# Gate tiles by GpSimd's indirect gathers instead of SyncE's broadcast reads, in a convolution, attention and mixture-of-experts kernel

## The chip, the cores and the metric

The kernel runs on one core of a Trainium2 chip. A core has TensorE (PE; its weight loads are PEld), VectorE (DVE), ScalarE (ACT), GpSimd (POOL) and SyncE (SP), which only issues transfers, and 16 DMA engines that carry them. Every engine works through its own queue in order. The metric is the device time of one execution in microseconds. All times and durations below come from the profile of one execution, or from the list of measured times.

## The reference, cut to what matters

The input is 32 images of 128 channels with 56 x 56 points, in float32. Layer 0 is a convolution of signs with a residual; layer 1 turns each image into 3136 tokens of 128 channels, adds a linear attention, and then a mixture of 8 experts of which each token uses the best two. The last of these is the part that the change touches:

```python
def _L1_ffn_ref(x, router_w, router_b, expert_w, expert_b):
    router_probs = jax.nn.softmax(x @ router_w + router_b, axis=-1)
    top_p, top_i = jax.lax.top_k(router_probs, K)          # K = 2 of E = 8
    top_p = top_p / jnp.sum(top_p, axis=-1, keepdims=True)
    expert_out = jnp.einsum('bnd,edc->bnec', x, expert_w) + expert_b
    gathered = jnp.take_along_axis(expert_out, top_i[..., None], axis=2)
    return jnp.einsum('bnk,bnkc->bnc', top_p, gathered)
...
x = x + _L0_conv_ref(_gn(x), ...)                          # 3x3 convolution of signs
t = _to_tokens(x)                                          # 32 x 3136 x 128
t = t + _L1_attn_ref(_ln_t(t), ...)                        # q * sum(k * v)
t = t + _L1_ffn_ref(_ln_t(t), ...)
```

## The kernel before, in words

The kernel multiplies every token by all 8 experts, each time with the token first scaled by its gate for that expert, which is zero for six of the eight. PE then adds the eight products in PSUM, and no token has to be sorted to its expert.

The tokens of an image are cut into 25 chunks of up to 128, and these into 7 blocks: five of 512 tokens, one of 384 and one of 192. The experts are taken in 4 pairs. So an image has 28 steps of one block and one pair each. Per step:

- `spread` (L670 on) fetches a gate tile `bc`: the gates of the block for the two experts, one row of up to 1024 numbers, repeated in all 128 partitions (the channels). For the first pair of a block it also fetches `gt`, the same gates in bfloat16 parts, for the experts' biases (L676).
- `gated` (L689) multiplies the block's tokens `tt` by the gate tile on DVE.
- `experts` (L701, L707) multiplies the result by the two experts' weights on PE and accumulates in the PSUM tile `ff`.
- `finish` (L718, L721) adds `ff` to the tokens and stores the output.

The gates come from a chain earlier in the image. The statistics of the tokens go through a reciprocal root on POOL (L278, in `rstd_of`), DVE builds the logits (L562) and picks the two largest, PE transposes the gates (L621), ACT copies them (`gt_sb`), and SP writes them to a buffer `gp` in device memory (L628), where each block and expert has a row of 512 numbers. `gate_parts` writes the bfloat16 parts to `gb` with seven transfers (L643). The `bc` tiles are read back from `gp`, with a source that names the same bytes for every partition.

The order of the work comes from a list: each step is put at a time measured in images (`at(when, ...)`), with the stages of three to four images overlapped, and the steps are issued sorted by that time. A scheduler then settles the order of every engine's instructions and adds the waits. The times that matter here: an image's gates are written at s + 2.17 to s + 2.19; its 28 gate tiles are asked for from s + 2.235 on, each at the earliest when the multiply seven steps before it has been asked for, because `bc` has seven buffers; its multiplies start at s + 2.30 and take one image's time.

POOL has four jobs. For each image it takes two reciprocal roots (L278: one for the attention's normalisation, whose result ACT needs for `y`, one for the experts', whose result the logits need); it sets a column of ones in the seven tiles `y` (L386), each of which waits until PE has finished with an older one; and it adds the attention's bias to the tokens (`bias`, L464 and L469: seven and one instructions) once DVE has computed it (`kv_4`, `bq_kv`, L434). DVE's additions of the projected queries (`tok`, L518) need those sums. POOL issues no transfers.

Of the kernel before, what the change touches and what calls it, by code (L numbers as in the profile page):

```python
# [41 lines left out]
C = 128  # L42
# [3 lines left out]
N_EXP = 8  # L46
# [10 lines left out]
def conv_attn_moe_kernel(  # L57
# [19 lines left out]
    nc = tc.nc  # L77
# [9 lines left out]
    while c0 < n_ck:  # L87
        left = n_ck - c0
        n = PER if left > PER + 1 else (left + 1) // 2 if left > 3 else left
        blocks.append(list(range(c0, c0 + n)))  # L90
        c0 += n
    n_blk = len(blocks)
# [6 lines left out]
    def cols_of(b):  # L99
        return blocks[b][0] * C, min(n_tok, (blocks[b][-1] + 1) * C)  # L100

    const = ctx.enter_context(tc.tile_pool(name="const", bufs=1))
# [56 lines left out]
    def by_slot(name, *shape):  # L159
        both = [const.tile([C, *shape], F32, name=f"{name}{j}") for j in range(2)]  # L160
        for t in both:
            nc.gpsimd.memset(t, 0.0)
        return both
# [3 lines left out]
    lgp_all = by_slot("lgp", n_slot, N_EXP)  # L167
    n_half = 2
    gate_all = by_slot("gate", 2, n_half * C // (N_EXP * PER), N_EXP, PER)
    move_all = [const.tile([C, N_Q], F32, name=f"move{j}") for j in range(2)]  # L170

    def load_x(i: int):
# [107 lines left out]
    def plan_image(i: int):  # L280
        s = float(i)
        d = {}
# [93 lines left out]
        for g in range(n_blk):  # L376
            b = min(n_conv - 1, (cols_of(g)[1] - 1) // (ROWS * width))
# [292 lines left out]
        def spread(b, k):  # L670
            n = cols_of(b)[1] - cols_of(b)[0]
            if k == 0:
                gt = bpool.tile([n_g, WIDE], BF16, tag="gt", name=f"gt_{i}_{b}")
                rows = d["gb"][b, :, :, :n].rearrange("j e t -> (j e) t")
                for r in range(0, n_g, n_g // 3):
                    nc.sync.dma_start(gt[r : r + n_g // 3, :n], rows)  # L676
                d["gt", b] = gt
            bc = bpool.tile([C, 2, WIDE], F32, tag="bc", bufs=7, name=f"bc_{i}_{b}_{k}")
            nc.sync.dma_start(
                bc[:, :, :n],  # L680
                d["gp"][b, 2 * k : 2 * k + 2, :n].unsqueeze(0).to_broadcast([C, 2, n]),
            )
            d["bc", b, k] = bc

# [45 lines left out]
        for b in range(n_blk):  # L730
            for k in range(pairs):
                n = b * pairs + k
                at(max(s + 2.235 + 0.001 * n, begin + (n - 7 + 0.1) * unit), spread, b, k)
                at(begin + n * unit, gated, b, k)
                at(begin + (n + 1.3) * unit, experts, b, k)
            at(begin + ((b + 1) * pairs + 1.0) * unit, finish, b)
# [54 lines left out]
```

## Time and profile before

| what | value |
|---|---|
| time of the kernel before, median of 2 runs | 2791.74 us (2788.21 to 2795.28) |
| the profiled execution: its own time | 2786.31 us |
| the profiled execution: its span | 2784.5 us |
| mean granted clock of TensorE | 0.975 |
| bytes moved | 544.86 MB in 251246 packets |
| share of the 16 DMA engines, queue of SP | 55.9% (538.07 MB) |
| L679, issue of `bc` on SP | 896 times, median 349 ns |
| L689, multiply by the gate tile on DVE | 896 times, mean 1149 ns |
| L707, expert matmuls on PE | 3584 times, mean 551 ns |
| L278, reciprocal root on POOL | 64 times, mean 5326 ns |
| L464, bias add on POOL | 224 times, mean 1885 ns |

The span is the time from the first to the last instruction. "Busy" is the time in which an engine has an instruction running; a busy PE need not be at its peak. A line that ends in "<- engine, tile, line" names what an idle engine was waiting for, as the profile infers it from the semaphores. Issuing a transfer isn't counted as busy time.

### The profile page before, as it was taken

How to read it: one execution, taken by the hardware profiler on the slowest of the kernel's cores; microseconds unless marked ns; L12 is line 12 of the kernel's file. 1: busy time of each engine (PE TensorE's matmuls, PEld its weight loads, DVE VectorE, ACT ScalarE, POOL GpSimd, SP SyncE). 2: the span in 40 equal slices, each digit the busy share in tenths (PEclk: the TensorE clock that was granted, in tenths of full speed). 3: DMA queues.
4: the chain of work that ended last, by engine and by line, in shares of the span. 5: the costliest groups of instructions: out<-in, count | busy, mean ns of one | idle time of the engine just before them, and what ended most of it. 6: DMA issues, size and time to landing. Idle time of an engine off the chain costs nothing. (4 is left out here: it accounts for less than half of the span.)

```text
span 2784.5 us, 35742 instructions
## 1 busy us (share of the span) xinstructions
PE 2539.2 (91%) x11149; PEld 1537.5 (55%) x11149; DVE 2164.8 (78%) x5049; ACT 938.9 (34%) x2473; POOL 807.4 (29%) x568
## 2 busy tenths in 40 slices
PE   4799999999999999999999999999999999999887
PEld 2655555555555555555555555555555555555553
DVE  3578877788877788777879777888777888777875
ACT  3532333433333333333333333323334323333210
POOL 1322232232332232331332331332331332331320
PEclk9899999999999999999999999999999999999999
DMA  3166555466555466554566654575554575654566
GB/s 134 35 223 232 205 200 181 169 226 228 209 197 186 162 231 220 211 186 170 192 234 210 216 185 160 200 242 200 209 188 163 210 242 201 209 185 139 190 219 227
DMA packets 251246, 544.86 MB, mean 196 GB/s; under 512 B 54377, under 2 KB 147889, under 8 KB 251057
## 3 DMA queue, kind: packets, MB, share of 16 engines
q1 hardware_dynamic: 247424, 538.07, 55.9%
q10 hardware_dynamic: 3632, 4.51, 0.5%
q8 instruction: 90, 1.47, 0.2%
q14 instruction: 100, 0.81, 0.1%
HBM read 481.38 MB, written 61.08 MB: 195 GB/s over the span
## 5 line engine op out<-in xcount | busy, mean ns | idle before, releaser
L707 PE MATMUL ff<-gated,ew_sb 128*128 128x512 f32 (+2 forms) x3584 | 1513.9, 551 | 65.9 <-DVE gated L689 65.6
L689 DVE TENSOR_TENSOR gated<-tt,bc 128x1024 f32<-128x1024 f32 (+2 forms) x896 | 1025.3, 1149 | 33.5 <-PE ff L707 17.6
L707 PEld LDWEIGHTS ff<-gated,ew_sb 128*128 128x128 f32 x3584 | 644.1, 193 | 516.1 <-issue 339.0
L278 POOL TENSOR_TENSOR r<-var,m_half 128x28 f32<-128x28 f32 x64 | 340.0, 5326 | 1085.8 <-DVE var L277 1021.5
L464 POOL TENSOR_TENSOR tok<-tok,bq_kv 128x512 f32<-128x512 f32 (+2 forms) x224 | 415.1, 1885 | 206.3 <-DVE bq_kv L434 206.3
L328 PE MATMUL cv<-xb,w_bin 128*128 128x448 bf16 x2016 | 450.2, 358 | 1.4 <-DVE lgp L519 1.1
L498 ACT ACTIVATE qs<-q,r 128x136 f32<-128x136 f32 (+1 forms) x800 | 241.9, 370 | 463.4 <-issue 280.3
L389 ACT ACTIVATE y<-tok,r 128x128 f32<-128x128 f32 (+1 forms) x800 | 255.3, 394 | 226.6 <-POOL r L278 216.1
L400 PE MATMUL gram<-y 128*128 128x129 f32 (+1 forms) x1600 | 254.0, 297 | 77.1 <-ACT y L389 76.8
L489 PEld LDWEIGHTS q<-move,x 128*128 128x128 f32 (+1 forms) x1600 | 228.9, 191 | 123.9 <-issue 78.2
L328 PEld LDWEIGHTS <-w_bin 128*128 128x128 bf16 x2016 | 197.9, 98 | 166.4 <-issue 22.7
L400 PEld LDWEIGHTS gram<-y 128*128 128x128 f32 (+1 forms) x1600 | 228.9, 203 | 105.8 <-ACT y L389 90.1
L489 PE MATMUL q<-move,x 128*128 128x144 f32 (+1 forms) x1600 | 249.9, 291 | 3.8 <-DVE lgp L519 2.5
L562 DVE TENSOR_TENSOR logit<-logit,r 128x224 f32<-128x224 f32 x32 | 12.6, 393 | 296.9 <-POOL y L386 255.0
L367 DVE BATCH_NORM_STATS2 st<-tok 128x6 f32<-128x128 f32 (+1 forms) x800 | 182.4, 280 | 25.9 <-ACT tok L358 25.6
L339 DVE SCALAR_TENSOR_TENSOR x<-cv,alpha_col,x 128x448 f32<-128x448 f32 x224 | 151.5, 676 | 65.1 <-PE cv L328 61.2
L386 POOL MEMSET y<- 128x4 f32 x224 | 23.1, 104 | 608.4 <-PE gram L400 450.4
L718 DVE TENSOR_TENSOR tt<-tt,ff 128x512 f32<-128x512 f32 (+2 forms) x224 | 137.3, 613 | 68.9 <-PE ff L707 66.7
L518 DVE TENSOR_TENSOR tok<-tok,qs 128x384 f32<-128x384 f32 (+1 forms) x320 | 159.5, 499 | 37.6 <-ACT qs L498 31.4
L527 DVE BATCH_NORM_STATS2 st<-tok 128x6 f32<-128x128 f32 (+1 forms) x800 | 183.1, 282 | 0.0
L358 ACT COPY tok<-xt 128x512 f32<-128x512 f32 (+2 forms) x224 | 117.9, 527 | 180.2 <-PE xt L354 180.0
L665 PEld LDWEIGHTS l<-ident,tok 128*128 128x128 f32 (+1 forms) x800 | 106.8, 149 | 100.9 <-issue 78.2
(115 smaller groups left out, 1636.1 us busy)
## 6 DMA issues: line engine op xcount, KB each, us to landing
bc<-gp SPq DMA_DIRECT2D x640, 512.0 KB
x<-in_x_dram SPq DMA_DIRECT2D x64, 784.0 KB
bc<-gp SPq DMA_DIRECT2D x128, 384.0 KB
out_dram<-tt SPq DMA_DIRECT2D x64, 512.0 KB
bc<-gp SPq DMA_DIRECT2D x128, 192.0 KB
out_dram<-tt SPq DMA_DIRECT2D x32, 448.0 KB
gt<-gb SPq DMA_DIRECT2D x480, 24.0 KB
gb<-gt_parts SPq DMA_DIRECT2D x224, 24.0 KB
```

The costliest lines, as they stand in the source:

```text
L278: nc.gpsimd.tensor_tensor(dst, var, m_half.to_broadcast([C, n_slot]), ALU.pow)
L328: nc.tensor.matmul(cv, lhsT=w_bin[:, t, :], rhs=xs[:, b * ROWS + dy : b * ROWS + dy + ROWS, dx : dx + width], start=(t == 0), stop=(t == T ...
L367: nc.vector.bn_stats(st[:n, slot[c], :], d["tok"][:n, c, :])
L389: nc.scalar.mul(y[:n, j, :C], d["tok"][:n, c, :], d["r1"][:n, slot[c] : slot[c] + 1])
L400: nc.tensor.matmul(d["gram"], lhsT=y[:n, j, :C], rhs=y[:n, j, :], start=(c == 0), stop=(c == n_ck - 1),)
L464: nc.gpsimd.tensor_tensor(t, t, over, ALU.add)
L489: nc.tensor.matmul(p[:n, k, :], lhsT=d["x"][:, c * C : c * C + n], rhs=move, start=True, stop=True,)
L498: nc.scalar.mul(qs[:n, k, :], p[:n, k, : C + N_EXP], d["r1"][:n, slot[c] : slot[c] + 1])
L518: nc.vector.tensor_add(t, t, qs[:n, k:m, :C])
L527: nc.vector.bn_stats(st2[:n, slot[c], :], d["tok"][:n, c, :])
L689: nc.vector.tensor_tensor(g[:, :, :n], d["tt"][:, lo:hi].unsqueeze(1).to_broadcast([C, 2, n]), d.pop(("bc", b, k))[:, :, :n], ALU.mult,)
L707: nc.tensor.matmul(d["ff", b][:, :n], lhsT=ew_sb[:, e * C : (e + 1) * C], rhs=g[:, j, :n], start=False, stop=(e == N_EXP - 1),)
```

## The change

The gate tile of a step is no longer read by SP with a repeating source. GpSimd issues an indirect gather in its place: each of the 128 partitions names the row of `gp` that it wants, and gets that row. `gp` is looked at as rows of 1024 numbers, one for each block and pair, so all 128 partitions name the same row. The row numbers stand in a new constant tile `row_no`, a column for each of the 28 steps, which POOL fills at the start. A gather fetches the whole row of 1024 numbers, also for the two shorter blocks, whose tiles were read with 2 x 384 and 2 x 192 numbers before. The number of buffers and the times at which the tiles are asked for stay. From the first insertion on, lines of the changed kernel have numbers higher by 4, and after the second by 7 (`gated` is at L696, `experts` at L708 and L714).

```diff
     gate_all = by_slot("gate", 2, n_half * C // (N_EXP * PER), N_EXP, PER)
+
+    row_no = const.tile([C, n_blk * N_EXP // 2], mybir.dt.uint32, name="row_no")
+    for n in range(n_blk * N_EXP // 2):
+        nc.gpsimd.memset(row_no[:, n : n + 1], n)
     move_all = [const.tile([C, N_Q], F32, name=f"move{j}") for j in range(2)]
...
             bc = bpool.tile([C, 2, WIDE], F32, tag="bc", bufs=7, name=f"bc_{i}_{b}_{k}")
-            nc.sync.dma_start(
-                bc[:, :, :n],
-                d["gp"][b, 2 * k : 2 * k + 2, :n].unsqueeze(0).to_broadcast([C, 2, n]),
+            n_pair = b * (N_EXP // 2) + k
+            nc.gpsimd.indirect_dma_start(
+                out=bc.rearrange("p j t -> p (j t)"),
+                out_offset=None,
+                in_=d["gp"].rearrange("b (k j) t -> (b k) (j t)", j=2),
+                in_offset=bass.IndirectOffsetOnAxis(ap=row_no[:, n_pair : n_pair + 1], axis=0),
             )
             d["bc", b, k] = bc
```

## The prediction

> **What bounds the kernel now.** I read the page's busy times first, then the waits, and then one image in the middle of the run, engine by engine.
>
> ```profile
> PE 2539.2 (91%) x11149; PEld 1537.5 (55%) x11149; DVE 2164.8 (78%) x5049; ACT 938.9 (34%) x2473; POOL 807.4 (29%) x568
> ```
>
> PE comes first. The 32 images overlap; the pairs of reciprocal roots on POOL (L278) start at 1028.16, 1111.46 and 1195.99 us, so one image takes about 84 us. POOL works 25.5 us of each. The stretches inside one image (columns: length, then busy time of PE, PEld, DVE, ACT, POOL with counts, PE clock, DMA share, GB/s):
>
> ```profile
> 1136.00:1147.00 11.00, 11.00 (x73) 8.56 (x73) 6.11 (x20) 2.24 (x6) 0.42 (x4) 1.00 0.58 167
> 1142.00:1152.00 10.00, 10.00 (x47) 5.90 (x47) 7.90 (x18) 1.44 (x3) 2.35 (x4) 1.00 0.90 287
> 1150.00:1164.00 14.00, 12.98 (x44) 6.45 (x43) 13.85 (x18) 1.14 (x5) 14.00 (x8) 1.00 1.03 387
> 1164.00:1195.00 31.00, 31.00 (x129) 17.72 (x128) 29.68 (x82) 12.32 (x32) 0.02 (x1) 1.00 0.60 203
> ```
>
> See three things. DVE is as full as PE from 1150 to 1195 (43.5 of 45 us), so what holds DVE up there holds up the image. DVE has a hole from 1136 to 1147, where the new image's gate tiles are on their way. From 1150 to 1164 POOL and the DMA engines are full too. The timeline of POOL for that image, with the idle time before each group in brackets:
>
> ```profile
> 1111.46 10.67 POOL L278 TENSOR_TENSOR r<-var,m_half 128x28 f32<-128x28 f32 x2 [31.97 <-DVE var L277]
> ...
> 1139.18 0.10 POOL L386 MEMSET y<- 128x4 f32 x1 [2.61 <-PE gram L400]
> ...
> 1149.86 13.44 POOL L464 TENSOR_TENSOR tok<-tok,bq_kv 128x512 f32<-128x512 f32 x7 [6.24 <-DVE bq_kv L434]
> 1163.26 0.76 POOL L469 TENSOR_TENSOR tok<-tok,bq_kv 64x128 f32<-64x128 f32 x1
> 1195.99 5.92 POOL L278 TENSOR_TENSOR r<-var,m_half 128x28 f32<-128x28 f32 x1 [31.97 <-DVE var L276]
> ```
>
> POOL has two free stretches, 1122 to 1150 and 1164 to 1196, with 14.2 us of bias adds between them. Its results are waited for:
>
> ```profile
> DVE logit L562 <- POOL y L386: 255.0, 27, 9.4
> ...
> DVE gated L689 <- DMA bc<-gp: 15.0, 14, 8.7
> ```
>
> The first is the wait for the roots (named after the memset behind them), 9.4 us an image. The second is all that DVE now loses to gate tiles that come late, 8.7 of its 15.0 us in the last image. SP's timeline shows why:
>
> ```profile
> 1136.05 0.39 SPq L628 DMA_DIRECT2D gp<-gt_sb  x1
> 1137.41 3.77 SPq L643 DMA_DIRECT2D gb<-gt_parts  x7
> 1141.28 1.14 SPq L676 DMA_DIRECT2D gt<-gb  x3
> 1142.47 1.77 SPq L679 DMA_DIRECT2D bc<-gp  x4
> ```
>
> The first gate tile is issued 6.4 us after gp, behind ten other issues.
>
> **What the Trainium skill says.** *DMA: Bandwidth & Descriptors*, "Latency and other measured facts", gives a DMA from GpSimd about 1 us to its first byte, put down to the descriptors that its cores emit, against 0.6 us from SP; its section "Anatomy of one DMA — SWDGE (gpsimd) path" fits a GpSimd DMA as 2.0 us plus bytes over 436 GB/s. No DMA here is issued on POOL, so the trace can't confirm it; on SP one issue takes 0.35 us, and in the last image the first gate tile, issued at 2726.55, is used at 2730.71, 4.2 us later, with three more behind it. *GPSIMD Engine Reference*, "Performance pitfalls for Q7 kernels", prices small reads such as one per gather index at about 102 cycles each. *SBUF — State Buffer*, "Who interferes with whom", says a VectorE instruction with two SBUF inputs contends with a GpSimd instruction that reads SBUF. The trace agrees: the seven bias adds take 8.17 us in the first image (85.45 us), when no gate multiply runs, and 13.44 us beside them, and a multiply takes up to 1.90 instead of 1.21 us there.
>
> **The change part by part.**
>
> *Removed from SP:* 28 issues an image, 28 x 0.35 = 9.8 us of SP, and their waits for a free buffer. Nothing waits for SP alone, so 0. The output stores and gt loads are no longer queued behind those waits: 0 to a few us in all, taken as 0.
>
> *Row numbers:* 28 memsets of one column at the start. Eight like them (L244) take 0.33 us, so about 1.2 us near 9 us, where POOL then idles until 66: 0. Without that cover, 1.2 us once.
>
> *Bytes:* a gather always fetches 4 KB a partition, also for the blocks of 384 and 192 columns: 28 x 512 = 14336 KB against 20 x 512 + 4 x 384 + 4 x 192 = 12544 KB, 1.84 MB more an image, 59 MB in all. These are the last eight gathers; at 387 GB/s they are 4.7 us of DMA time in a stretch where the engines are 0.60 busy: 0.
>
> *Emission on POOL, the unknown.* Call it E for one gather of 128 rows. Low end: 0.35 us, SP's row. High end: 128 x 102 cycles at 1.2 GHz, an estimate from the GPSIMD page, 10.9 us, if the row numbers are read one by one. The DMA page's 1 us is for a plain DMA; this one must also read 128 row numbers, one in each partition, while VectorE uses two inputs. I take E = 1.5 us and keep 0.8 to 2.6 for the range. POOL's sum is 25.5 + 28 x 1.5 = 67.5 of 84 us: it fits on average, and is full at E = (84 - 25.5) / 28 = 2.1 us. What matters is the order on the queue.
>
> *POOL's new order in an image:* the two roots; the last gather of the image before; the memsets of y, the last of which ends at 1139.3; gathers 0 to 10; two bias adds; gather 11; the other bias adds; gathers 12 to 26 with two memsets between; the next two roots. Gather n waits until multiply n - 7 has freed its buffer. I replay this on the old times. gp, issued at 1136.05, has landed by 1139.3 (the same fit gives its 128 KB 2.3 us). Multiplies 0 to 3 end early enough that gathers 7 to 10 hardly wait, so gather 10 ends at 1139.3 + 11E. The bias inputs (L434, ready at 1149.8 now) come some 4 us later, since DVE's new order puts six gate multiplies ahead of kv (L431), still before 1155.8. Two adds, gather 11, the other adds and gather 12: 1139.3 + 13E + 14.2. With the page's 2.0 us and 524288 bytes at 436 GB/s (3.2 us), tile 12 is there at 1156.7 + 13E. Multiply 12 (block 3, first pair) starts at 1173.30 now. At E = 1.28 it is just in time; at 1.5 it lands at 1176.2, 2.9 us late. DVE has 1.3 us of idle time up to 1195; the other 1.6 us reach the roots, and through them y and PE. PE's own lead over this tile hides only its direct wait. Later gathers need one tile in about 2.9 us and catch up.
>
> *The roots wait behind gather 26*, which waits for multiply 19 (ends 1194.4, root input ready 1195.9): 1194.4 + 1.5 = 1195.9, so 0 now; each further us of E goes into the 9.4 us wait. DVE's logit, ACT's y and then PE's gram wait for that.
>
> *Contention:* a multiply beside POOL's reads grew by up to 0.69 us. If every gather did that, 28 x 0.69 = 19 us an image; if it reads only its numbers, 0. I take 1 us.
>
> *Early start:* gather 0 starts at 1139.3 instead of 1142.47. DVE's new order fills its hole with these multiplies, but PE is full there and the chain through kr (L444, L445) ends as late as before, so I count 0 in the middle. At the end nothing covers: 3 us are gained once.
>
> Sum: 1.6 + 1.0 = 2.6 us an image, over the 31 images with a successor 81 us, less 3: 2786.31 + 78 = 2864 us in terms of the profiled execution (span 2784.5 and 1.8 around it). The median of the runs shown is 5.4 above that one, so I forecast 2869.
>
> **The rivals.**
>
> *POOL becomes the bound.* From E = 2.1 on POOL has no free time, and the late tile shows sooner: at E = 2.6, tile 12 lands at 1190.5, 17 us late, and POOL's sum is 98.3 us an image: 14.3 to 17 us x 31, 3230 to 3310 us. At 2.1 it is 10.7 - 1.3 = 9.4 us an image, 3080. For: POOL issues in order, bias and roots are waited for. Against: 71% of POOL is idle.
>
> *Emission is short, and the early start pays.* One mechanism: tile 0 leaves SP's queue of ten issues behind it. It decides where E is at most 1.2, so that tile 12 is in time. Then up to 65.6 us of PE's waits for a gate multiply (46 times) and the 15.0 us of DVE can go; half of that, 40 us, gives 2752, the whole 2711. For: DVE's hole and the full DMA engines after it. Against: PE's work is 79 of 83.5 us already.
>
> *The transfer is hidden either way.* With E from 1.2 to 1.35 the lateness fits into DVE's idle 1.3 us and the numbers cancel: about 2790, within the 2% that a measurement of this kernel can tell from no change.
>
> *It isn't one descriptor a row:* if rows are cut into smaller pieces, emission is several times longer and the first rival holds with 4000 us and more.
>
> **How the numbers follow.** Forecast (E 1.35 to 1.9; 2815 to 3030): 0.42. POOL the bound: 0.24, with pieces 0.03. Hidden: 0.22. Early start: 0.09, of which 0.05 are faster by over 2%. Slower by over 2% gathers the forecast's upper 0.40 and 0.27: 0.67; within 2%: 0.28; faster: 0.05. The range leaves out about a tenth at each end: 2760 to 3240.
>
> **What would show it.** Gathers on POOL at about 1.5 us; a bias group that starts near 1156 and is split by one gather; idle time of DVE before multiply 12 for a DMA, some 2 to 3 us an image; DVE's wait for the roots no longer than 9.4 us; no SP issues of bc. I am wrong if E is under 1.2 or over 2, if the multiplies lengthen much beyond 1.21 us, or if gathers land slower than 3.2 us after emission.

## The result, and the profile after

The changed kernel takes 2978.85 us (median of 2 runs, 2978.28 to 2979.41) against 2791.74 us (2788.21 to 2795.28). The ratio is 1.067, with a 95% interval of 1.061 to 1.073: 187 us slower, 6 us an image. The forecast was 2869 us, 78 us slower: the sign and the range were right, the size was not. The profiled execution took 2978.28 us, with a span of 2976.5 us, 192 us longer than before. One execution of one experiment below (the product of `gt` last) ran in a slow state, 4195 us at a mean clock of 0.585, and is left out of that experiment's median.

The page of the changed kernel, its engines' busy times and the groups of the gathers and of the multiplies (busy us and mean ns, then the idle time before them):

```profile
PE 2583.9 (87%) x11149; PEld 1558.6 (52%) x11149; DVE 2245.8 (75%) x5049; ACT 940.3 (32%) x2473; POOL 1730.9 (58%) x1492
...
L684 POOL DMA_INDIRECT bc<-gp,row_no x896 | 1087.1, 1213 | 689.7 <-DVE gated L696 348.1
L696 DVE TENSOR_TENSOR gated<-tt,bc 128x1024 f32<-128x1024 f32 (+2 forms) x896 | 1145.9, 1283 | 223.3 <-DMA bc<-gp,row_no 114.2
```

PE executes the same 11149 instructions, but is busy 44.7 us longer; the mean granted clock fell from 0.975 to 0.962. The other 147 us of the longer span are idle time of PE. DVE executes the same 5049 instructions and is busy 81 us longer. One image in four stretches (length, busy time of PE, PEld, DVE, ACT, POOL, then PE clock, DMA share and GB/s):

```profile
1127.00:1142.00 15.00, 12.63 (x54) 7.42 (x53) 9.33 (x16) 0.85 (x2) 12.03 (x10) 1.00 0.91 293
1142.00:1155.00 13.00, 10.25 (x42) 5.35 (x41) 12.96 (x15) 1.72 (x6) 12.56 (x11) 1.00 0.53 190
1155.00:1189.00 34.00, 34.00 (x144) 19.34 (x143) 32.32 (x89) 12.34 (x32) 17.27 (x17) 1.00 0.79 259
1189.00:1200.00 11.00, 8.00 (x32) 5.62 (x30) 0.93 (x3) 5.76 (x14) 10.80 (x4) 0.84 0.41 167
```

The stretch that the forecast worried about, the long one from 1155 on, is the healthy one: PE is full there. PE has its holes in the first 28 us, while the gathers and then the bias adds run, and at the roots, where the clock falls too. POOL's timeline for this image, with the idle time before each instruction in brackets:

```profile
1127.00 0.94 POOL L684 DMA_INDIRECT bc<-gp,row_no  x1 [0.99 <-DMA gp<-gt_sb]
1128.24 0.94 POOL L684 DMA_INDIRECT bc<-gp,row_no  x1 [0.30 <-issue]
...
1143.53 2.50 POOL L468 TENSOR_TENSOR tok<-tok,bq_kv 128x512 f32<-128x512 f32 x2
1146.18 1.76 POOL L684 DMA_INDIRECT bc<-gp,row_no  x1 [0.16 <-issue]
1147.97 5.07 POOL L468 TENSOR_TENSOR tok<-tok,bq_kv 128x512 f32<-128x512 f32 x5
1153.00 1.42 POOL L473 TENSOR_TENSOR tok<-tok,bq_kv 64x128 f32<-64x128 f32 x1
1154.58 0.96 POOL L684 DMA_INDIRECT bc<-gp,row_no  x1 [0.16 <-issue]
...
1187.19 2.18 POOL L684 DMA_INDIRECT bc<-gp,row_no  x1 [0.30 <-DVE gated L696]
1189.39 4.82 POOL L282 TENSOR_TENSOR r<-var,m_half 128x28 f32<-128x28 f32 x1
```

A gather takes 0.94 us when nothing disturbs it, with 0.30 us to the next. The five bias adds after 1147.97 are of three sizes; those of 128x512 take 1.27 us each, where in the kernel before the median of this size was 2.24 us. DVE at the same time:

```profile
1147.95 6.16 DVE L696 TENSOR_TENSOR gated<-tt,bc 128x1024 f32<-128x1024 f32 x1
```

One multiply, which takes 1.21 us elsewhere, takes 6.16 us: it starts with the first of POOL's six adds and ends 1.1 us after the fifth. In the kernel before, the adds run one behind the other too (13.44 us for seven), but there is no such multiply; there adds and multiplies took turns. POOL's first two adds of that image ran from 1149.86 to 1152.04 and from 1152.00 to 1154.25, and each multiply below ends 1.1 us after one of them:

```profile
1151.22 1.90 DVE L689 TENSOR_TENSOR gated<-tt,bc 128x1024 f32<-128x1024 f32 x1
...
1153.44 1.90 DVE L689 TENSOR_TENSOR gated<-tt,bc 128x1024 f32<-128x1024 f32 x1
```

And what PE waits for in the changed kernel (total us, times, longest):

```profile
PE gram L404 <- ACT y L393: 112.1, 49, 4.7
PE l L669 <- ACT tt L672: 34.8, 27, 1.8
PE ff L708 <- DMA gt<-gb: 34.4, 16, 12.6
...
PE ff L708 <- issue: 19.0, 11, 4.3
```

The wait for `gt`, the experts' bias gates, was 6.9 us in all before. Here it is 34.4, and 19.0 more stand before the same matmul. The wait for `y`, which hangs on the roots, was 76.8 us.

### The profile page after: what moved, and what is told of

Same layout as the page of the kernel before. It is cut to its first block, busy times and chain, and to the rows that moved or that the text cites. A ratio compares the mean times of both kernels' runs of the same rounds, so it can differ in the third digit from the quotient of the medians.

```text
span 2976.5 us, 36136 instructions
## 1 busy us (share of the span) xinstructions
PE 2583.9 (87%) x11149; PEld 1558.6 (52%) x11149; DVE 2245.8 (75%) x5049; ACT 940.3 (32%) x2473; POOL 1730.9 (58%) x1492
## 3 DMA queue, kind: packets, MB, share of 16 engines
q0 software_dynamic: 129024, 469.82, 46.3%
## 4 chain that ended last, share of the span: by engine, by line
PE 44%; DVE 18%; ACT 12%; POOL 9%; issue 9%; DMA 8%; SPq 1%; another core or an unknown queue 0%; DVEq 0%; ACTq 0%; POOLq 0%
PE ff L714 23%; DVE gated L696 8%; PE cv L332 8%; POOL r L282 6%; PE q L493 5%; DMA bc<-gp,row_no 4%; ACT y L393 4%; PE gram L404 3%; POOL bc L684 3%; ACT xb L297 3%; ACT qs L502 2%; DMA gt<-gb 2%; DVE tok L522 2%; PE xt L358 2%; ACT xb L313 1%
## 5 line engine op out<-in xcount | busy, mean ns | idle before, releaser
L714 PE MATMUL ff<-gated,ew_sb 128*128 128x512 f32 (+2 forms) x3584 | 1541.9, 557 | 30.7 <-DVE gated L696 17.6
L684 POOL DMA_INDIRECT bc<-gp,row_no x896 | 1087.1, 1213 | 689.7 <-DVE gated L696 348.1
L696 DVE TENSOR_TENSOR gated<-tt,bc 128x1024 f32<-128x1024 f32 (+2 forms) x896 | 1145.9, 1283 | 223.3 <-DMA bc<-gp,row_no 114.2
L714 PEld LDWEIGHTS ff<-gated,ew_sb 128*128 128x128 f32 x3584 | 658.0, 197 | 483.8 <-issue 387.0
L332 PE MATMUL cv<-xb,w_bin 128*128 128x448 bf16 x2016 | 433.8, 356 | 1.0 <-DVE lgp L523 0.8
L404 PE MATMUL gram<-y 128*128 128x129 f32 (+1 forms) x1600 | 264.9, 301 | 112.3 <-ACT y L393 112.1
L282 POOL TENSOR_TENSOR r<-var,m_half 128x28 f32<-128x28 f32 x64 | 306.8, 4805 | 72.0 <-DVE var L281 71.4
L404 PEld LDWEIGHTS gram<-y 128*128 128x128 f32 (+1 forms) x1600 | 236.8, 208 | 149.0 <-ACT y L393 127.2
L468 POOL TENSOR_TENSOR tok<-tok,bq_kv 128x512 f32<-128x512 f32 (+2 forms) x224 | 261.5, 1198 | 44.9 <-DVE bq_kv L438 44.0
L669 PE MATMUL l<-ident,tok 128*128 128x128 f32 (+1 forms) x800 | 142.2, 297 | 35.1 <-ACT tt L672 34.8
```

Of the source, the lines that this page charges most:

```text
L282: nc.gpsimd.tensor_tensor(dst, var, m_half.to_broadcast([C, n_slot]), ALU.pow)
L332: nc.tensor.matmul(cv, lhsT=w_bin[:, t, :], rhs=xs[:, b * ROWS + dy : b * ROWS + dy + ROWS, dx : dx + width], start=(t == 0), stop=(t == T ...
L404: nc.tensor.matmul(d["gram"], lhsT=y[:n, j, :C], rhs=y[:n, j, :], start=(c == 0), stop=(c == n_ck - 1),)
L468: nc.gpsimd.tensor_tensor(t, t, over, ALU.add)
L684: nc.gpsimd.indirect_dma_start(out=bc.rearrange("p j t -> p (j t)"), out_offset=None, in_=d["gp"].rearrange("b (k j) t -> (b k) (j t)", j= ...
L696: nc.vector.tensor_tensor(g[:, :, :n], d["tt"][:, lo:hi].unsqueeze(1).to_broadcast([C, 2, n]), d.pop(("bc", b, k))[:, :, :n], ALU.mult,)
```

## The experiments

In each run the kernel before was timed beside the others; its medians were 2789.55 to 2792.35 us. Times below are medians, ratios are against it. "Held" is DVE's time above the usual duration (the median of the same instruction in the kernel before without the bias adds), summed over all of DVE's instructions that are over it by 0.2 us or more: 121 us before, 218 us after the change, 0 in both kernels without the adds.

### The bias adds: one at a time, and none

In the changed kernel, one gather's step between any two bias adds:

```diff
+        unit_b = 1.0 / (n_blk * N_EXP // 2)
-            at(s + 1.445 + 0.001 * g, bias, g)
+            at(s + 1.445 + unit_b * g, bias, g)
```

> The changed kernel, with the bias adds of an image set one unit apart, so that a gather stands between any two of them on POOL; nothing else is edited. Theory A (the group of five bias adds holds one gate multiply for about 5 us, in 31 images): the multiplies of 6.2 to 6.6 us go, none is over 3 us, and the time falls by 100 to 155 us, to 2825 to 2880. Theory B (DVE and PE wait at the start of an image for tiles that DVE's new order puts first): the long multiplies may go, but PE's work only moves up to the next wait, and the time stays within 25 us of 2979. Theory C (POOL's queue is too slow with 28 gathers, and roots and tiles come late): no change or slower, since each gather behind a bias add now starts later: 2970 to 3020.

Measured: 2908.96 us, ratio 1.043 (1.040 to 1.046), 70 us less than the change alone, which lies between the numbers of theories A and B: the adds are one cost of several. POOL now does what the edit says:

```profile
1108.05 1.27 POOL L468 TENSOR_TENSOR tok<-tok,bq_kv 128x512 f32<-128x512 f32 x1
1109.48 1.84 POOL L685 DMA_INDIRECT bc<-gp,row_no  x1 [0.16 <-issue]
1111.34 1.27 POOL L468 TENSOR_TENSOR tok<-tok,bq_kv 128x512 f32<-128x512 f32 x1
```

No multiply is longer than 3 us any more (33 were, 167 us above the usual in sum), and DVE is held for 167 us. So the run of adds costs about 70 us, a bit over a third of the change.

Then both kernels with the adds left out, so that the tokens are not given the attention's bias:

```diff
-            at(s + 1.445 + 0.001 * g, bias, g)
+            pass
```

> The changed kernel without the bias adds on POOL (they are left out; their vector is zero with these inputs). Theory A: no multiply is over 3 us, 2800 to 2860. Theory B: 2940 to 2980, since the start of an image is as before. Theory C: POOL is relieved of 9 us an image, so part of the loss goes: 2880 to 2940.

> The kernel before without the bias adds on POOL, as the other end of the pair. All theories: its multiplies are lengthened by 115 us in all beside the bias adds, and DVE is full in that stretch, so it gains something: 2740 to 2790. Theory A: the difference to the changed kernel without them is at most 60 us. Theories B and C: it is at least 120 us.

Measured: 2837.22 us (1.016, 1.013 to 1.019) for the changed kernel and 2720.30 us (0.975, 0.973 to 0.977) for the one before. Nothing on DVE is held in either. They are 117 us apart instead of 187: the adds carry 70 us of the change, as the spread found by another way, and 117 us have to do with something else.

The same spread in the kernel before was meant as a control.

> Control: the spread of the bias adds in the kernel before, where no multiply is longer than 3 us and the excess over 1.21 us is 61 us in all. If the 70 us that the spread wins in the changed kernel are the price of the long multiplies that only the change brings: 2780-2800 us here. If the spread is simply a better place for these adds: 2720-2745 us.

Measured: 2788.70 us, 0.9992 (0.998 to 1.000). It wins nothing there, but it is no control either. POOL has nothing else on its queue at that place, so the adds still run one behind the other:

```profile
1153.37 13.44 POOL L464 TENSOR_TENSOR tok<-tok,bq_kv 128x512 f32<-128x512 f32 x7 [6.24 <-DVE bq_kv L434]
```

That the 70 us come with the change rests on the pair without the adds.

### The form and the bytes of the transfers

The kernel before, its broadcast reads unchanged but issued by GpSimd:

```diff
-            nc.sync.dma_start(
+            nc.gpsimd.dma_start(
                 bc[:, :, :n],
```

> The kernel before with its broadcast reads issued on POOL as they are, not as indirect gathers: no row numbers are read, and the two short blocks fetch only their own columns (59 MB less than the changed kernel). Theory A: the long multiply stays, as the order on POOL is the same, and so does the time: 2940 to 2990. If reading the row numbers is what holds VectorE, the multiplies return to 1.21 us and the time to 2800 to 2860. If the added bytes matter, it falls by 20 us or more with the long multiplies still there.

Measured: 2913.25 us, 1.044 (1.042 to 1.046). An issue takes 0.59 us on POOL instead of 1.21, DVE is held for 197 us, with 31 multiplies over 3 us, and PE waits 92.6 us for `gt`. So moving the reads to GpSimd's queue costs 123 us, two thirds of the change, without any gather. POOL is busy 41% of the span here.

The kernel before with its reads at full width in blocks 5 and 6, as the gathers read them:

```diff
-                bc[:, :, :n],
-                d["gp"][b, 2 * k : 2 * k + 2, :n].unsqueeze(0).to_broadcast([C, 2, n]),
+                bc,
+                d["gp"][b, 2 * k : 2 * k + 2, :].unsqueeze(0).to_broadcast([C, 2, WIDE]),
```

> The kernel before with its broadcast reads at full width in blocks 5 and 6 too, as the gathers read them: 59 MB more, issued by SyncE as before. If bytes cost nothing: 2783-2800 us. If the 66 us between the changed kernel and the plain DMAs on GpSimd's queue are those bytes: 2840-2860 us.

Measured: 2788.61 us, 0.9987 (0.998 to 1.000). On SP's queue the 59 MB are free. On GpSimd's queue they were not tried alone, so of the 66 us between the plain DMAs and the gathers it stays open what the bytes have and what the form has.

### The late gt

In the changed kernel, the product of `gt` as the last of a block's accumulation instead of the first:

```diff
-                nc.tensor.matmul(
-                    d["ff", b][:, :n], lhsT=eb_w, rhs=d.pop(("gt", b))[:, :n], start=True, stop=False
-                )
...
-                    start=False,
-                    stop=(e == N_EXP - 1),
+                    start=(e == 0),
+                    stop=False,
                 )
+            if k == N_EXP // 2 - 1:
+                nc.tensor.matmul(
+                    d["ff", b][:, :n], lhsT=eb_w, rhs=d.pop(("gt", b))[:, :n], start=False, stop=True
+                )
```

> Theory L (the gate parts' tile gt lands late behind the early gathers, and TensorE stands before the first product of a block): with gt's product last in the block nothing waits for it early, the 53 us of waits for gt fall to under 10, and the time falls by 35 to 60 us, to 2920-2945 us. Rival (the wait is only where the slack of that stage shows, and the next wait takes its place): the waits for gt vanish too, but others of TensorE grow by as much, and the time stays within 12 us of 2979.

Measured: 2912.76 us, 1.042 (1.039 to 1.045), 66 us less. The waits for `gt` are gone from the list. The control in the kernel before:

> The same edit of the product of gt in the kernel before, where the trace shows 6.9 us of waits for gt: both theories expect 2783 to 2800 us, no difference from before. If it comes out over 20 us faster, the gain of the edit in the changed kernel is not the price of the change.

Measured: 2783.16 us, 0.9975 (0.997 to 0.999): 6 us less. These are not its one wait for `gt`, for PE's idle time grew by 15 us; its busy time fell by 18.5 us, at a mean clock of 0.987 instead of 0.975. In the changed kernel the edit took 51 us of idle time and 14.5 us of busy time. So the late `gt` is the second cost that comes with the change, about 60 us. SP's queue in the changed kernel:

```profile
1123.35 1.13 SPq L632 DMA_DIRECT2D gp<-gt_sb  x1
1124.58 3.29 SPq L647 DMA_DIRECT2D gb<-gt_parts  x7
1127.97 2.38 SPq L680 DMA_DIRECT2D gt<-gb  x6
```

Before, the reads of `bc` stood on this queue behind `gb` and the first `gt`. Now the first gather starts at 1127.00, as soon as `gp` has landed and a microsecond ahead of the first `gt`; this is so in 27 of the 30 images in the middle of the run, and in none before. `gt` is not issued later: its first transfer follows `gp` by 4.5 us in the median, 4.8 before. But its product starts 4.6 us after the last of its three transfers was issued, in 26 of the 30 images after a wait, against 3.3 us before, without any wait. So it is the landing that is late. That the gathers' bytes hold it back is argued and not shown: gathers of 512 KB keep the DMA engines 0.91 busy while the small transfers of 24 KB are on their way, and in the kernel before the stretch with the same transfers had 0.58.

### Both edits together

> Both edits in the changed kernel, the bias adds spread (-70 us alone) and gt's product last in its block (-66 us alone). If the long multiplies and the late gt are separate costs, paid one after the other: 2979 - 136 = 2843, range 2830-2857 us. Rival (they share a cause, since both lie in the first quarter of an image and a wait that goes is taken up by the next): 2875-2910 us.

Measured: 2852.70 us, 1.021 (1.019 to 1.024), 126 us less than the change alone. The two edits add up to within 10 us, so these are two costs. The same two edits in the kernel before:

> Control: both edits in the kernel before (gt's product last alone gave 2783). If both causes belong to the change: 2775-2795 us. If the edits help everywhere: 2715-2745 us, and then the distance between the two ways to fetch is over 110 us still.

Measured: 2784.58 us, 0.998 (0.997 to 0.999). The adds stay in one run here too (13.43 us for seven), so this is the kernel with `gt` last once more. Between the two ways to fetch, 68 us stay. To see whether these are still the adds, both kernels with `gt` last and with the bias adds left out:

> The changed kernel with the bias adds left out (so tok is not given its bias) and gt's product last in a block. If the late gt is the whole of what is left without the adds: 2705-2735 us, level with the next kernel. If something beyond the adds and gt is left (the gathers' own place and pace): 2837 - 66 = 2771, range 2755-2790 us.

> The kernel before with the bias adds left out and gt's product last: 2720 without the second edit, which wins 6 us with the adds in place: 2705-2722 us by every theory.

Measured: 2786.61 us (0.9985, 0.998 to 1.000) and 2714.09 us (0.972, 0.971 to 0.974), 73 us apart. The rest has nothing to do with the adds or with `gt`'s place.

### The roots

Gathers 25 and 26 run just ahead of the two roots and take 2.3 and 2.2 us there in the median, beside DVE's work. In the changed kernel gathers 24 to 26 are queued behind the roots:

```diff
-        nc.gpsimd.tensor_tensor(dst, var, m_half.to_broadcast([C, n_slot]), ALU.pow)
+        root.append(nc.gpsimd.tensor_tensor(dst, var, m_half.to_broadcast([C, n_slot]), ALU.pow))
...
+            behind = 24 <= b * (N_EXP // 2) + k <= 26 and root
+            with tc.issue_after(root[-1].ins) if behind else nullcontext():
                 nc.gpsimd.indirect_dma_start(
...
-                at(max(s + 2.235 + 0.001 * n, begin + (n - 7 + 0.1) * unit), spread, b, k)
+                first = 2.985 if 24 <= n <= 26 else 2.235 + 0.001 * n
+                at(max(s + first, begin + (n - 7 + 0.1) * unit), spread, b, k)
```

> Theory R (gathers 24 to 26 run just ahead of the two roots on GpSimd and take 2 to 5 us beside VectorE's work, and the gram's first products and the routing wait for the roots): with these three gathers queued behind the roots the time falls by 1 to 1.6 us an image, 30 to 50 us, to 2930-2950 us, and TensorE's wait gram <- y falls from 112 us towards the 77 us of the kernel before. Rival (the roots' delay is hidden, and gathers 24 to 26 now land later in their stead): within 12 us of 2979, or slower by up to 25.

Measured: 2970.47 us, 1.063 (1.059 to 1.067), 8 us less, which its four executions (2955.70 to 2983.53 us) do not tell from the change alone. The same on top of the two edits:

> Both edits in the changed kernel (2853 us) and gathers 24 to 26 behind the roots. Theory R (the roots' delay is what is left, hidden behind the other two causes when it was taken away alone): 2805-2830 us, and TensorE's gram <- y falls from 81 us to 46-55. Rival (the delay of the roots is off the path): 2843-2863 us.

Measured: 2883.79 us, 1.034 (1.030 to 1.039), 31 us more than without it. The wait for `y` did go, from 80.7 to 47.1 us, but PE waits for `tt` instead:

```profile
PE l L670 <- ACT tt L673: 92.2, 29, 3.5
PE gram L405 <- ACT y L394: 47.1, 63, 4.6
```

The wait for `tt` was 58.1 us without the edit. The theory that the roots' delay is the rest is wrong.

### The order at the start of an image

In the changed kernel the scheduler puts the first multiplies ahead of `prod` and `kv` on DVE. This edit puts multiplies 0, 1 and 2 back behind `prod`, `kv` and `bq_kv`:

```diff
+            ahead[i, 1] = nc.vector.tensor_add(kv, n_bkbv, d["kv_ps"])
...
+            behind = ahead.get((i + 1, k)) if b == 0 else None
+            with tc.issue_after(behind.ins) if behind else nullcontext():
                 nc.vector.tensor_tensor(
...
-                at(begin + n * unit, gated, b, k)
-                at(begin + (n + 1.3) * unit, experts, b, k)
+                at(max(begin + n * unit, s + 2.441 + 0.002 * n), gated, b, k)
+                at(max(begin + (n + 1.3) * unit, s + 2.442 + 0.002 * n), experts, b, k)
```

> Theory O (the planner moves the first five or six multiplies and their experts ahead of the prod/kv chain on VectorE and ahead of cv_3, kv_ps and xt_2 on TensorE, and VectorE then stands for gathers that a later place would have covered): with multiplies 0, 1 and 2 ordered behind prod, kv and bq_kv as in the kernel before, VectorE's 114 us of waits for bc fall by more than half and the time falls by 30 to 60 us, to 2920-2950 us. Rival (order at the start of an image is free): 2965-2995 us.

Measured: 3068.10 us, 1.100 (1.097 to 1.103), 89 us more. DVE's waits for `bc` fell from 114 to 42 us, as expected, but DVE is held for 243 us, and 55 instructions are over 2 us above the usual (33 after the change): `kr` (L452, 8 numbers in each partition) now falls into the run of adds as well. With the adds spread and `gt` last:

> All three edits in the changed kernel. If long multiplies, late gt and the order at the start of an image make up the whole change: 2785-2815 us, level with the kernel before (2790). If the order is worth nothing: within 15 us of the kernel with the first two edits. If there is a further cost of the gathers themselves on GpSimd (the delayed roots, the slots that 1.2 us gathers take): 2820-2860 us.

Measured: 2865.61 us, 1.027 (1.022 to 1.033), 13 us more than without the order. DVE's waits for `bc` are down to 23.2 us from 136.3, and it wins nothing. This theory is wrong too.

### The edits on plain DMAs

> Both edits on the plain DMAs of 0.6 us from GpSimd's queue (2913 us alone). If what is left is the 1.2 us that an indirect gather holds GpSimd: 2785-2810 us. If it is the place on GpSimd's queue whatever the form: 2840-2865 us. If the kernel with these edits and the gathers behind the roots (2923 us) tells of the edits themselves: 2900-2930 us.

> Broadcast reads issued by GpSimd as plain DMAs (2913 us alone), with the bias adds spread (-70 us in the changed kernel), gt's product last and gathers 24 to 26 behind the roots. If the three causes are separate and are paid by the reads' place on GpSimd's queue: 2913 - 66 - 50 - 30, 2750 to 2790 us, level with the kernel before. If they overlap, or what is left belongs to the new order at the start of an image: 2820 to 2870 us.

Measured: 2914.42 us (1.045, 1.043 to 1.047) with the two edits, and 2923.12 us (1.048, 1.046 to 1.050) with the gathers behind the roots as well. What won 126 us with the indirect gathers wins nothing here. In the first of the two, POOL alternates an add and a DMA of 0.57 us:

```profile
1027.61 0.57 POOL L679 DMA_DIRECT2D bc<-gp  x1
1028.20 1.27 POOL L464 TENSOR_TENSOR tok<-tok,bq_kv 128x512 f32<-128x512 f32 x1
1029.41 0.57 POOL L679 DMA_DIRECT2D bc<-gp  x1
1030.00 1.27 POOL L464 TENSOR_TENSOR tok<-tok,bq_kv 128x512 f32<-128x512 f32 x1
1031.20 0.57 POOL L679 DMA_DIRECT2D bc<-gp  x1
```

DVE meanwhile, and then PE:

```profile
1027.81 3.81 DVE L445 TENSOR_SCALAR kr<-kr,bq_col 128x8 f32<-128x8 f32 x1
...
1031.67 0.59 PE L451 MATMUL kr_ps<-kr,ones 128*128 128x8 f32 x2 [3.54 <-DVE kr L445]
```

No long multiply is left, but the instruction that is held is now `kr`, through two adds and the issue between them, 105.8 us in the whole run, and PE waits 103.5 us for it. Two spread adds with a short issue between them held DVE like a run. With the 1.8 us of a gather between them (the first experiment), `kr` was not held: 0.5 us in the whole run.

### What the rest is made of

The profiles show where it goes. PE's timeline in the changed kernel at a root, and then two stretches of 2 us there, whose third column from the end is PE's clock:

```profile
1106.19 2.43 PE L404 MATMUL gram<-y 128*128 128x129 f32 x8 [3.00 <-ACT y L393]
```

```profile
1104.00:1106.00 2.00, 0.00 (x0) 0.00 (x0) 0.00 (x0) 0.27 (x1) 2.00 (x2) 0.99 0.48 195
1106.00:1108.00 2.00, 1.81 (x7) 1.54 (x8) 0.00 (x0) 2.00 (x8) 2.00 (x1) 0.50 0.02 6
```

The same place in the kernel before, where eight such matmuls take 1.06 us at full clock (1122.58 us):

```profile
1117.86 1.07 PE L400 MATMUL gram<-y 128*128 128x129 f32 x6 [1.96 <-ACT y L389]
```

```profile
1117.00:1119.00 2.00, 1.07 (x6) 0.88 (x6) 0.00 (x0) 1.59 (x5) 2.00 (x2) 1.00 0.48 199
```

After 1.96 us of waiting PE runs on at full clock. After 3.00 us it runs at half clock, and eight matmuls take 2.43 us. The length of the wait alone doesn't decide this: in the kernel before, 16 of the 30 waits of 1.75 to 2.0 us were followed by half clock within 3.4 us, and 14 were not. What goes with it is in the clock record. In all 20 traces the granted clock is either full or half, and its changes lie on a grid of 3.41 us, to within 6 ns. The table takes each window of this grid from 70 us on in which the clock was full, and sorts them by PE's idle time inside the window.

| idle time of PE in a window of 3.41 us | windows in the 20 traces | next window at half clock |
|---|---|---|
| under 1.2 us | 13613 | 1 |
| 1.2 to 2.0 us | 1121 | 213 |
| 2.0 us and more | 547 | 546 |

The wait of 1.96 us lay across a line of the grid (1117.04), with 1.14 us on one side and 0.82 us on the other. Of the wait of 3.00 us, 2.78 us lay in one window, and the clock is half from the next line (1105.97) on. The next table counts over six traces, from 70 us on: PE's waits of 2 us and more, the sum of its waits, the times that the clock fell, and the time that the missing clock amounts to.

| kernel | PE's waits of 2 us and more | all waits, us | falls of the clock | (1 - clock) x time, us | PE busy, us |
|---|---|---|---|---|---|
| before | 19 | 203 | 33 | 68 | 2539.2 |
| changed | 47 | 349 | 51 | 114 | 2583.9 |
| before, both edits | 8 | 217 | 11 | 35 | 2520.7 |
| changed, both edits | 25 | 246 | 37 | 77 | 2562.2 |
| before, no adds, gt last | 7 | 167 | 8 | 24 | 2499.3 |
| changed, no adds, gt last | 26 | 206 | 33 | 74 | 2539.3 |

Idle and busy time account for the whole change: 147 us more of idle time and 45 us more of busy time make the 192 us of span. In the last pair, where adds and `gt` are out of the way, 40 of the 77 us of span are the same PE instructions at a lower clock; the other 37 are waits, of which `y` has 33 (75.1 against 42.1 us). With both edits it is 41.5 of 71 us. So more than half of the rest is the clock that is lost after longer waits of PE. Which single cause makes those waits stays open: taking away the one for `y` brought up one for `tt`. The gathers' place and pace on POOL may be behind all of them, but no run here separates it.

## Why the prediction was right or wrong

*What bounds the kernel:* right for the place, wrong in what it left out. PE and DVE are full from 1155 to 1189, and nothing was lost there. The time went in the stretch that the prediction called a hole.

*Removed from SP, row numbers, bytes:* each was put at 0. For bytes this is shown on SP's queue: 2788.61 us with all of them. The row numbers are 28 POOL memsets at the start, 0.98 us in all, under the same cover. SP's issues went, but "gt loads are no longer queued behind those waits" had the wrong end in view: these loads had been protected by standing ahead of the `bc` reads on the same queue.

*Emission:* right. 1.21 us of busy time and 0.30 to the next is the 1.5 us that was taken, from a range of 0.8 to 2.6.

*POOL's new order, tile 12:* this step failed; it was the largest term, 1.6 us an image or 50 us. The bias group was split by one gather, as forecast, and came 20 us after `gp`'s issue (1123.35 to 1143.53). But it took 9 us of adds, not the 14.2 us of the old trace, since the adds no longer took turns with the multiplies, and gather 12 was out at 1155.54, 32.2 us after `gp`; the replay had it at 37 us. Its multiply starts 41.6 us after `gp` (at 1164.90), and ran without a wait. DVE's waits for `bc` come at the first tiles instead: in images 1 to 30 the first five have all 108 us of them. The first tile's multiply, where it waited, began 3.85 us after the gather's issue had ended (median of 21), the second tile's 5.6 us (of 16). That is slower than the 3.2 us that the prediction took, and one of its own signs of being wrong.

*Contention:* the kind of cost was right, the pair of instructions and the size were not. It was taken as 1 us an image, 31 us, of a range of 0 to 19 us an image. DVE is held 96 us more, 3.1 us an image, and the run of adds costs 70 us. The price came from the wrong pair: not a gather beside a multiply, but the bias adds, which in the changed kernel hold one multiply through five of them.

*Early start:* this step failed most. It was 0 in the middle of the run and 3 us won at the end. The gathers do start early, ahead of the first `gt`, and PE loses about 60 us (51 us in the changed kernel without adds) to 24 KB transfers whose landing the prediction never priced.

*The roots behind gather 26:* DVE's wait for them rose from 9.4 us an image to about 10.5 (324 us in 31 waits, the longest 11.7), because two gathers take over 2 us there: with them behind the roots it was 9.3 us. As forecast this reaches `y` and PE, but taking it away won 8 us at the most.

*The sum* of 81 us had no term for the clock: waits were priced at their length, but PE's busy time for the same instructions grew by 44.7 us. That is a quarter of the change, and part of the costs above, not beside them. Nor had it a term for the late `gt`, about 60 us of the 187; 70 us are the run of adds, and the cause of the rest, near 60 us, stays open.

*The rivals:* POOL doesn't become the bound, at 58% busy. "The early start pays" had the chain right and the sign wrong. "Hidden" was right for bytes only. The 128 rows did not cost more pieces: 129024 packets on the gathers' queue are 144 for a gather, about one for a row.

The prediction took the contention from the Trainium skill's *SBUF — State Buffer*, "Who interferes with whom", which says that a VectorE instruction with two SBUF inputs contends with a GpSimd instruction that reads SBUF. It also says, of VectorE's two-port modes, that whichever of the two engines issues first has the shared pair for the whole instruction, and the other is blocked for that long. If this held for the multiply too, it would wait for one add, 1.27 us (an estimate from that page and the trace's add). The trace shows 6.16 us, through five adds, and 3.81 us for `kr`, through two adds and the issue between them, so waiting for one instruction is not the limit; here the measurement decides. For the clock, *TensorE: Matmul & The Clock Gate*, "HAM oscillation — how this bites in real kernels", warns of idle gaps over about 3.4 us. The direction agrees; in these traces less was enough, 2 us of idle time within one window of 3.41 us, and here the measurement decides.

## What to carry to other kernels

When a transfer moves to a queue of its own, list what stood ahead of it on the old one: its place in line may have been what kept a small, urgent transfer on time. Moving issues onto GpSimd also changes when its other work runs beside VectorE's, and a run of its elementwise instructions can hold one VectorE instruction through five of them, so look at the longest instruction of a group and not only at the mean. Price a TensorE wait at its length and, where it brings TensorE's idle time in one window of the clock's 3.41 us grid to about 2 us, at the half-clock time after it too.

## What was unexpected in the hardware

- One VectorE multiply of 1.21 us was held for 6.16 us while GpSimd executed five adds; this happened once in nearly every image (31 multiplies took 6.16 to 6.57 us, two 3.9 us). Before, with the same adds and multiplies, none was over 3 us, and a 128x512 add took 2.24 instead of 1.27 us in the median. What makes the two engines take turns in one case and not in the other stays open.
- A `kr` instruction on 8 numbers for each partition was held for 3.81 us in the same way, although a plain DMA issue of 0.57 us stood between the two adds.
- An indirect gather of 128 rows of 4 KB takes GpSimd 0.94 us when undisturbed, 1.21 us on the mean and 0.30 us to the next; a plain DMA that fills the same tile takes 0.59 us.
- TensorE's granted clock changes on a grid of 3.41 us, and 2 us of idle time within one window were enough for half clock in the next (546 of 547 windows); under 1.2 us almost never were (1 of 13613). A wait of 1.96 us can cost nothing more or a window at half clock, by where it lies on the grid.
- `gt` last in the kernel before lengthens PE's idle time by 15 us and still wins 6 us (2783.16 us, 0.25% less, 0.15 to 0.34%): the clock fell 11 times instead of 33, since of 43 waits of 1.75 to 2.5 us 2 are left.
